# Reordering the first stage of a graph layer: two products held back, signs in halves, adj halves moved ahead, loads gated later

## The chip, the cores and the metric

The kernel runs on one core of a Trainium2 chip. The metric is the device time of one execution in microseconds (us), the median of three runs. Beside it stands one profiled execution, whose trace gives each instruction's start and length on TensorE (PE, with its weight loads PEld), VectorE (DVE), ScalarE (ACT), GpSimd (POOL) and SyncE (SP), and each transfer's issue and landing.

## The reference

Two graph layers over 4096 nodes with 512 features each. Only the first layer's product is touched by the change:

```python
def _L0_gnn_ref(x, support, weight):
    bw = _bin_sign(weight)            # sign
    ba = _bin_sign_z(x)               # max(sign, 0)
    xw = ba @ bw.T
    out = support @ xw                # support is adj, 4096 x 4096
    return jax.nn.relu(out)
...
x = _layernorm(x + _L0_gnn_ref(x, adj, L0_gnn_weight), axis=-1)
x = _layernorm(x + _L1_gnn_ref(x, adj, L1_gnn_weight, L1_gnn_bias, L1_gnn_node_w, L1_gnn_edge_w), axis=-1)
```

The second layer is an attention layer: h = x @ edge_w, a masked softmax over h @ h.T, and the product of adj times that attention with x @ weight.

## The kernel before

The 4096 nodes are cut into 32 row blocks of 128 (NB) and into 8 groups (NG) of 512 nodes, that is of four blocks (BG). The first layer runs in two stages. The second layer (from about 490 us on) uses a seven-product scheme for its large products and a planner for its own order; nothing of it is changed.

The first stage, up to about 55 us, builds xw, and meanwhile TensorE already uses each finished part of xw for two output row blocks, 0 and 4 (the list `early`), in the two accumulators acc 0 and acc 1. Its steps for a group g are these:

- `load_x(g)` (L182 to L186) loads the transposed x of the group, 1 MB, on SP's queue. `load_a(g, n)` (L188 to L193) loads adj of the group against early block n, 256 KB, on the same queue. For some of them a one-element memset on VectorE writes the tile first, so that the load must wait until VectorE has come that far in its own order.
- `signs_x(g)` makes the 0/1 signs on VectorE. Two blocks share one number: `over` is 2^11 for a positive element of the later block (L201), and `ba` is the sign of the earlier block plus that (L204). For group 0 this goes quarter by quarter as x and w0 land (L212, L213, and L210 for the weight's signs on ScalarE).
- `product(g, j)` multiplies ba by the weight's signs, four matmuls (L225). One product serves two blocks, j and j + 2.
- `taken(g, j)` separates the two by adding and taking away a large constant: L232 on ScalarE (us), L234 on VectorE (xw of block j), L235 on ScalarE (xw of block j + 2).
- `split(g, n)` splits adj of half n into hi, rounded to fp32r on ScalarE (L243), and lo, the rest, on VectorE (L244). hi and lo tiles have two buffers each, and one pair of tiles holds both halves of a group.
- `follow(g, n, cs)` adds hi times xw and lo times xw to acc n for the blocks cs of the group (L250, L252), two matmuls for each block.

For VectorE, ScalarE and TensorE the order of the program is the order in which these calls are written out by hand. SP's queue is in the hands of the framework's scheduler, which puts a load as early as its waits let it, so SP's order is not the written one. The loads draw on pools: adj halves on `rows` with four buffers, x on `stream` with three (w0 holds one at first).

After the stage, L308 and L310 load two vectors, node_w and bias, as tiles nw_b and bias_b of 128 partitions: each partition reads the same 2 KB row. They are used from 59 us on. The second stage then runs over the other 30 row blocks, each with 64 matmuls (L450, L451), the hi and lo split of its adj rows (L440, L442), and the layer norm of finished blocks between.

The written order of the first stage around the change is this (before the loop over g, then the loop):

Of the kernel before, what the change touches and what calls it, by code (L numbers as in the profile page):

```python
# [15 lines left out]
ALU = mybir.AluOpType  # L16
AX = mybir.AxisListType

P = 128
# [3 lines left out]
TWO = 2.0**11  # L23
# [6 lines left out]
def kernel(  # L30
# [13 lines left out]
    nc = tc.nc  # L44
# [114 lines left out]
    with (  # L159
# [19 lines left out]
        halves = [slice(h * (W // 2), (h + 1) * (W // 2)) for h in range(2)]  # L179

        def load_x(g):
            xts[g] = stream.tile([P, KD, W], F32, name="xt", tag="stream")  # L182
            if g == 1:
                nc.vector.memset(xts[g][:, 0, 0:1], 0.0)
            if g:
                nc.sync.dma_start(xts[g], x_t[:, ts(g, W)].rearrange("(k p) n -> p k n", p=P))  # L186

        def load_a(g, n):  # L188
            a = rows.tile([P, BG, P], F32, name="a0", tag="rows")
            if not g and n:  # L190
                nc.vector.memset(a[:, 0, 0:1], 0.0)
            nc.sync.dma_start(a, adj_t[early[n], :, ts(g, BG), :])
            split_a[g, n] = a  # L193

        def signs_x(g):
            xt = xts.pop(g)
            ba = wp.tile([P, KD, W // 2], F32R, name="ba", tag="quarter", bufs=2)
            over = wp.tile([P, KD, W // 2], BF16, name="over0", tag="scr")
            rights_s[g] = ba
            if g:  # L200
                nc.vector.tensor_scalar(over, xt[:, :, halves[1]], 0.0, TWO, ALU.is_gt, ALU.mult)  # L201
                yield
                for j in range(2):
                    nc.vector.scalar_tensor_tensor(  # L204
                        ba[:, :, ts(j, P)], xt[:, :, ts(j, P)], 0.0, over[:, :, ts(j, P)], ALU.is_gt, ALU.add
                    )
                    yield
                return
            for k in range(KD):
                nc.scalar.activation(bw[:, k, :], w0[:, k, :], AF.Sign, scale=-1.0)  # L210
                a, b = (xt[:, k, h] for h in halves)
                nc.vector.tensor_scalar(over[:, k, :], b, 0.0, TWO, ALU.is_gt, ALU.mult)  # L212
                nc.vector.scalar_tensor_tensor(ba[:, k, :], a, 0.0, over[:, k, :], ALU.is_gt, ALU.add)  # L213
                yield

        def zeros(n):
            for _ in range(n):
                nc.tensor.matmul(idle, warm[:, :P], warm, start=True, stop=True)
# [3 lines left out]
        def product(g, j):  # L222
            pw = pws[g, j] = ps_mm.tile([P, D], F32, name="pw", tag="mm")
            for k in range(KD):
                nc.tensor.matmul(pw, rights_s[g][:, k, ts(j, P)], bw[:, k, :], start=(k == 0), stop=(k == KD - 1))  # L225
                if g == 0 and (not j or k == KD - 1):
                    zeros(2)

        def taken(g, j):
            pw = pws.pop((g, j))  # L230
            u = us[:, j, :]
            nc.scalar.activation(u, pw, AF.Identity, bias=shift[:, 0:1])  # L232
            b = g * BG + j
            nc.vector.scalar_tensor_tensor(xw[:, b, :], u, SHIFT, pw, ALU.subtract, ALU.subtract)  # L234
            nc.scalar.activation(xw[:, b + BG // 2, :], u, AF.Identity, bias=shift[:, 1:2], scale=-1.0 / TWO)  # L235

        def split(g, n):
            if not n:
                hi = sp.tile([P, QC, P], F32R, name="hi", tag="hi")
                lo = sp.tile([P, QC, P], F32R, name="lo", tag="lo")  # L240
                split_a[g] = hi, lo
            (hi, lo), a = split_a[g], split_a.pop((g, n))
            nc.scalar.copy(hi[:, ts(n, BG), :], a)  # L243
            nc.vector.tensor_sub(lo[:, ts(n, BG), :], a, hi[:, ts(n, BG), :].bitcast(F32))  # L244

        def follow(g, n, cs=(0, 2, 1, 3), apart=False):
            hi, lo = split_a[g]
            for c in cs:
                kb = g * BG + c
                nc.tensor.matmul(accs[n], hi[:, n * BG + c, :], xw[:, kb, :], start=(kb == 0), stop=False)  # L250
                if not apart:
                    nc.tensor.matmul(accs[n], lo[:, n * BG + c, :], xw[:, kb, :], start=False, stop=(kb == NB - 1))  # L252
            for c in cs if apart else ():
                kb = g * BG + c
                nc.tensor.matmul(accs[n], lo[:, n * BG + c, :], xw[:, kb, :], start=False, stop=False)

        with tc.manual_schedule(
            engines={mybir.EngineType.DVE, mybir.EngineType.Activation, mybir.EngineType.PE}
        ):
            load_x(0)  # L260
            for k in range(KD):
                nc.sync.dma_start(w0[:, k, :], w0_t[ts(k, P), :])
                nc.scalar.dma_start(xts[0][:, k, :], x_t[ts(k, P), :W])
            load_a(0, 0)
            nc.scalar.activation(us[:, 0, 0:1], eps, AF.Sign)
            idle = ps_mm.tile([P, D], F32, name="idle", tag="mm")
            accs.extend(ps_tr.tile([P, D], F32, name="acc0", tag="tr") for _ in early)
            zeros(WARM)
            for k, _ in enumerate(signs_x(0)):
                if k == 1:  # L270
                    load_a(0, 1)
                    load_x(1)
            product(0, 0)
            split(0, 0)
            taken(0, 0)
            product(0, 1)
            split(0, 1)
            taken(0, 1)
            for _ in signs_x(1):
                pass  # L280
            follow(0, 0, (0, 2))
            follow(0, 1, (0, 2), True)
            follow(0, 0, (1, 3))
            follow(0, 1, (1, 3))
            for g in range(NG - 1):
                if g:
                    follow(g, 0)
                for n in range(2):
                    load_a(g + 1, n)
                if g + 2 < NG:  # L290
                    load_x(g + 2)
                for j in range(2):
                    product(g + 1, j)
                if g:
                    follow(g, 1)
                ahead = signs_x(g + 2) if g + 2 < NG else iter(())
                split(g + 1, 0)
                taken(g + 1, 0)
                next(ahead, None)
                taken(g + 1, 1)  # L300
                for _ in ahead:
                    pass
                split(g + 1, 1)
            for n in range(2):
                follow(NG - 1, n)

# [1291 lines left out]
    over = big.tile([P, KD * N], F32, name="over", tag="large")  # L1598
# [129 lines left out]
```

## Time and profile before

| what | us |
|---|---|
| median of 3 runs (1912.49 to 1913.65) | 1913.15 |
| the profiled execution | 1913.24 |
| its span, from first to last instruction | 1911.4 |
| TensorE busy in it | 1898.2 |
| VectorE busy | 1456.9 |
| ScalarE busy | 1024.4 |
| first product with adj (L250) | 12.24 |
| first product of the second stage (L450) | 55.49 |

The span is 1.84 us shorter than the execution's time; what is before the first and after the last instruction is in the difference. The granted clock of TensorE is 0.999 over the span. A row of a timeline gives an instruction's start, its length, engine, line and tiles, and in brackets how long the engine had been idle before it and what it had waited for. A matmul's length is longer than its distance to the next one, because matmuls overlap. A transfer's time is from its issue on the queue to the landing of its last byte.

### The profile page before, as it was taken

How to read it: one execution, taken by the hardware profiler on the slowest of the kernel's cores; microseconds unless marked ns; L12 is line 12 of the kernel's file. 1: busy time of each engine (PE TensorE's matmuls, PEld its weight loads, DVE VectorE, ACT ScalarE, POOL GpSimd, SP SyncE). 2: the span in 40 equal slices, each digit the busy share in tenths (PEclk: the TensorE clock that was granted, in tenths of full speed). 3: DMA queues.
4: the chain of work that ended last, by engine and by line, in shares of the span. 5: the costliest groups of instructions: out<-in, count | busy, mean ns of one | idle time of the engine just before them, and what ended most of it. 6: DMA issues, size and time to landing. Idle time of an engine off the chain costs nothing.

```text
span 1911.4 us, 20674 instructions
## 1 busy us (share of the span) xinstructions
PE 1898.2 (99%) x6886; PEld 1234.3 (65%) x6886; DVE 1456.9 (76%) x2230; ACT 1024.4 (54%) x1647; POOL 310.4 (16%) x449
## 2 busy tenths in 40 slices
PE   9999999999999999999999999999999999999998
PEld 6888888888644555555555556666666666656646
DVE  7777677776866567686864887898879988898947
ACT  6433333333212567666777656666676567667731
POOL 0133132231421111111110111111111111110100
PEclk9999999999999999999999999999999999999999
DMA  9889898898595378577784877887777877787731
GB/s 320 298 323 357 306 342 325 324 360 309 183 303 204 123 290 319 187 255 274 293 320 152 322 287 287 288 296 285 275 276 285 295 276 276 264 308 265 282 114 55
DMA packets 143914, 520.94 MB, mean 273 GB/s; under 512 B 15040, under 2 KB 15040, under 8 KB 136128
## 3 DMA queue, kind: packets, MB, share of 16 engines
q1 hardware_dynamic: 64368, 235.43, 36.2%
q0 software_dynamic: 67632, 248.54, 34.0%
q10 hardware_dynamic: 11808, 35.66, 5.1%
q8 instruction: 54, 0.88, 0.2%
q14 instruction: 52, 0.43, 0.1%
HBM read 397.93 MB, written 121.63 MB: 272 GB/s over the span
## 4 chain that ended last, share of the span: by engine, by line
PE 94%; DVE 3%; issue 1%; ACT 1%; DMA 1%; ACTq 0%; POOL 0%; POOLq 0%; DVEq 0%
PE bank L1279 36%; PE seven L869 12%; PE acc L450 11%; PE acc L451 11%; PE pe L733 6%; PE seven L101 5%; PE po L1429 4%; PE pt L695 3%; PE inner L832 2%; PE acc L250 1%; PE pt L410 1%; PE acc L252 1%; PE pw L225 1%; PE bank L1429 0%; DMA s_d<-slot 0%
## 5 line engine op out<-in xcount | busy, mean ns | idle before, releaser
L1279 PE MATMUL bank<-lent,lop 128*128 128x256 f32 (+1 forms) x1496 | 483.3, 473 | 0.3
L1279 PEld LDWEIGHTS bank<-lent,lop 128*128 128x128 f32 x1496 | 283.8, 190 | 167.4 <-issue 140.1
L450 PE MATMUL acc<-xw,hi 128*128 128x512 f32 x960 | 376.4, 392 | 0.0
L451 PE MATMUL acc<-xw,lo 128*128 128x512 f32 x960 | 374.1, 390 | 0.0
L1279 PE MATMUL bank<-slot,lop 128*128 128x512 f32 (+1 forms) x800 | 286.6, 503 | 1.0 <-DVE slot L1060 0.6
L440 ACT CAST hi<-at 128x1024 fp32r<-128x1024 f32 x120 | 126.5, 1054 | 203.2 <-PE acc L450 146.7
L1279 PEld LDWEIGHTS bank<-slot,lop 128*128 128x128 f32 x800 | 151.5, 190 | 115.9 <-issue 101.4
L1290 ACT COPY over<-bank 128x512 f32<-128x512 f32 x200 | 116.2, 585 | 200.0 <-PE bank L1279 196.0
L451 PEld LDWEIGHTS acc<-xw,lo 128*128 128x128 f32 x960 | 180.3, 188 | 36.8
L450 PEld LDWEIGHTS acc<-xw,hi 128*128 128x128 f32 x960 | 180.2, 188 | 36.8
L442 DVE TENSOR_TENSOR lo<-at,hi 128x1024 fp32r<-128x1024 f32 x120 | 147.6, 1230 | 66.3 <-ACT hi L440 65.9
L733 PE MATMUL pe<-hT 128*128 128x512 f32 (+3 forms) x384 | 132.1, 486 | 0.0
L657 DVE CUSTOM_DVE_ANT_0 line<-lent,slot 128x512 f32<-128x512 bf16 x140 | 90.3, 688 | 54.9 <-ACT slot L696 29.0
L666 ACT ACTIVATE line<-line,nmax_c 128x512 f32<-128x512 f32 x160 | 114.7, 722 | 21.2 <-DVE nmax_c L657 20.8
L1441 DVE SCALAR_TENSOR_TENSOR xb<-po,f,xb 128x256 f32<-128x256 f32 x84 | 40.3, 480 | 74.8 <-PE po L1429 74.7
L733 PEld LDWEIGHTS pe<-hT 128*128 128x128 f32 x384 | 64.6, 191 | 41.4 <-issue 33.8
L1048 DVE CUSTOM_DVE_ANT_1 lent<-lent,line 128x2048 f32<-128x2048 f32 x39 | 88.7, 2283 | 0.0
L1252 ACT COPY bank<-over 128x512 f32<-128x512 f32 x144 | 86.7, 603 | 0.0
L695 PEld LDWEIGHTS pt<-ident,lent 128*128 128x128 f32 x418 | 52.4, 141 | 44.8 <-issue 34.8
L1051 ACT ACTIVATE lent<-lent 128x2048 f32<-128x2048 f32 x39 | 74.9, 1920 | 7.9 <-DVE lent L1048 7.6
L1054 ACT ACTIVATE slot<-slot 128x2048 f32<-128x2048 f32 x37 | 71.1, 1923 | 7.6 <-DMA slot<-in_adj_t_dram 7.6
L696 ACT COPY slot<-pt 128x512 f32<-128x512 f32 (+3 forms) x123 | 68.3, 556 | 12.3 <-PE pt L695 12.2
(297 smaller groups left out, 3019.0 us busy)
## 6 DMA issues: line engine op xcount, KB each, us to landing
lop<-lop_d SPq DMA_DIRECT2D x154, 512.0 KB, 4.5
at<-in_adj_t_dram SPq DMA_DIRECT2D x60, 1024.0 KB, 7.3
slot<-in_adj_t_dram POOLq DMA_DIRECT2D x39, 1024.0 KB, 8.0
lent<-s_d POOLq DMA_DIRECT2D x38, 1024.0 KB, 7.8
s_d<-slot POOLq DMA_DIRECT2D x30, 1024.0 KB, 8.9
lent<-in_adj_t_dram POOLq DMA_DIRECT2D x25, 1024.0 KB, 8.0
lent<-in_adj_dram SPq DMA_DIRECT2D x48, 512.0 KB, 4.9
s_d<-lent POOLq DMA_DIRECT2D x48, 512.0 KB, 6.1
```

The source lines that it names most:

```text
L101: nc.tensor.matmul(banks[bank][q], lop(m, q)[k], rop(m)[k], start=(first and k == 0), stop=(k == K - 1), skip_group_check=not first,)
L440: nc.scalar.copy(hi, aq)
L442: nc.vector.tensor_sub(lo, aq, hi.bitcast(F32))
L450: nc.tensor.matmul(acc, hi[:, c, :], xw[:, kb, :], start=(kb == 0), stop=False)
L451: nc.tensor.matmul(acc, lo[:, c, :], xw[:, kb, :], start=False, stop=(kb == NB - 1))
L657: nc.vector.tensor_tensor_reduce(line, mask, src, -1.0, HUGE, ALU.add, ALU.min, accum_out=nmax_c[:, b, c : c + 1])
L666: nc.scalar.activation(line, line, AF.Exp, bias=nmax_c[:, b, c : c + 1], scale=-1.0, accum_out=sum_c[:, b, c : c + 1])
L695: nc.tensor.transpose(pt[:, j, :], src[:, ts(j, P)], ident)
L733: nc.tensor.matmul(pe[:, lo * P :], hT[:, k, ts(A * BG + i, P)], hT[:, k, (B * BG + lo) * P : (B + 1) * W], start=(k == 0), stop=(k == KD ...
L869: nc.tensor.matmul(ps, left[m][:, k, q, :], right[m][:, k, :], start=(first and k == 0), stop=(k == KD // 2 - 1), skip_group_check=not first,)
L1279: nc.tensor.matmul(ps, lop[:, k, :], rop[:, k, :], start=start, stop=(k == K - 1), skip_group_check=True)
L1290: nc.scalar.copy(self.to(), self.bank[:, : self.w])
```

## The change

Five things change, all in the first stage.

1. In `load_a`, the memset that gates a load is now written for adj half 1 of group 0 and for adj half 0 of group 1 (`g + n == 1`), before for the first of these alone. Both adj loads of group 1 are written together with `load_x(1)`, after the third quarter of group 0's signs; `load_x(1)` stood after the second quarter, and the adj loads of group 1 stood in the loop.
2. For the groups after the first, `signs_x` makes `over` in two halves of 4 x 128 elements, each just ahead of the half of ba that uses it, instead of one of 1024.
3. The last block of group 0 on acc 1 (two matmuls, hi and lo) comes behind group 1's sign products instead of ahead of them.
4. Group 1's products are reordered: block 0 of acc 1 comes between the pairs (0, 2) and (1, 3) of acc 0, and the rest of acc 1 follows after group 2's sign products in the order 2, 1, 3.
5. Both halves of group 1's adj are split ahead of `taken(1, 0)`; for the other groups half 1 stays behind `taken(g, 1)`.

```diff
         def load_a(g, n):
             a = rows.tile([P, BG, P], F32, name="a0", tag="rows")
-            if not g and n:
+            if g + n == 1:
                 nc.vector.memset(a[:, 0, 0:1], 0.0)
             nc.sync.dma_start(a, adj_t[early[n], :, ts(g, BG), :])
...
             if g:
-                nc.vector.tensor_scalar(over, xt[:, :, halves[1]], 0.0, TWO, ALU.is_gt, ALU.mult)
-                yield
                 for j in range(2):
+                    nc.vector.tensor_scalar(
+                        over[:, :, ts(j, P)], xt[:, :, ts(2 + j, P)], 0.0, TWO, ALU.is_gt, ALU.mult
+                    )
+                    if not j:
+                        yield
                     nc.vector.scalar_tensor_tensor(
...
             for k, _ in enumerate(signs_x(0)):
                 if k == 1:
                     load_a(0, 1)
+                elif k == 2:
                     load_x(1)
+                    for n in range(2):
+                        load_a(1, n)
...
-            follow(0, 1, (1, 3))
+            follow(0, 1, (1,))
             for g in range(NG - 1):
+                if g == 1:
+                    follow(1, 0, (0, 2))
+                    follow(1, 1, (0,))
+                    follow(1, 0, (1, 3))
+                elif g:
+                    follow(g, 0)
                 if g:
-                    follow(g, 0)
-                for n in range(2):
-                    load_a(g + 1, n)
+                    for n in range(2):
+                        load_a(g + 1, n)
                 if g + 2 < NG:
                     load_x(g + 2)
                 for j in range(2):
                     product(g + 1, j)
-                if g:
-                    follow(g, 1)
+                follow(g, 1, {0: (3,), 1: (2, 1, 3)}.get(g, (0, 2, 1, 3)))
                 ahead = signs_x(g + 2) if g + 2 < NG else iter(())
                 split(g + 1, 0)
+                if not g:
+                    split(1, 1)
                 taken(g + 1, 0)
                 next(ahead, None)
                 taken(g + 1, 1)
                 for _ in ahead:
                     pass
-                split(g + 1, 1)
+                if g:
+                    split(g + 1, 1)
```

## The prediction

> **What bounds the kernel now.** I read the page's head first, then busy time by stretch, then the first stretch instruction by instruction on TensorE, VectorE, ScalarE and SP's queue, and last the transfers with their landings. Head, and busy time by stretch (stretch, length, then busy us and count of PE, PEld, DVE, ACT, POOL, then granted clock, DMA share, GB/s):
>
> ```profile
> PE 1898.2 (99%) x6886; PEld 1234.3 (65%) x6886; DVE 1456.9 (76%) x2230; ACT 1024.4 (54%) x1647; POOL 310.4 (16%) x449
> ```
> ```profile
> 0.00:12.24 12.24, 9.43 (x30) 3.86 (x30) 4.67 (x16) 6.06 (x10) 0.74 (x6) 1.00 0.84 303
> 12.24:24.66 12.42, 11.70 (x50) 8.97 (x49) 10.02 (x16) 8.51 (x14) 0.00 (x0) 1.00 1.05 387
> 24.66:55.27 30.61, 30.61 (x137) 25.34 (x136) 23.91 (x38) 20.46 (x33) 0.00 (x0) 1.00 0.94 313
> ```
>
> TensorE is the bound of the program, and from 24.66 us on it has no gap in the stage that is changed. Holes lie only before. TensorE's timeline where they are (start, length, what, idle before and its releaser):
>
> ```profile
> 16.08 1.98 PE L225 MATMUL pw<-bw,ba 128*128 128x512 f32 x8
> 18.66 0.50 PE L250 MATMUL acc<-xw,hi 128*128 128x512 f32 x1 [0.60 <-DVE xw L234]
> 19.47 0.40 PE L252 MATMUL acc<-xw,lo 128*128 128x512 f32 x1
> 19.99 0.50 PE L250 MATMUL acc<-xw,hi 128*128 128x512 f32 x1
> 24.66 0.39 PE L250 MATMUL acc<-xw,hi 128*128 128x512 f32 x1
> ```
>
> Matmuls in a run start 0.227 us apart (eight in 1.81 us on the chain). Between 12.24, the first product with adj, and 24.66, the first of follow(2, 0), stand 48 matmuls: 48 x 0.227 = 10.88 us of the 12.42. **1.54 us is all that reordering could give back there**, 0.08% of the span. The two waits above are most of it: 0.76 us until xw of group 1's first pair (start 18.66 against 16.08 + 1.81 = 17.90) and 0.29 until the second (19.99 against 19.70). What 12.24 itself waits for is the start-up loads of x and w0, the last landing at 2.15 + 7.2 = 9.35 on the chain.
>
> The transfers decide the rest. SP's queue up to 14 us, and two stretches of DMA, 8 to 12 us and 42 to 43 us:
>
> ```profile
> 4.54 2.58 SPq L192 DMA_DIRECT2D a<-in_adj_t_dram  x3
> 7.21 0.38 SPq L186 DMA_DIRECT2D xt<-in_x_t_dram  x1
> 7.64 0.53 SPq L192 DMA_DIRECT2D a<-in_adj_t_dram  x1
> 38.67 0.42 SPq L308 DMA_DIRECT2D nw_b<-in_node_w_dram  x1
> ```
> ```profile
> DMA packets 825, 1.56 MB, mean 391 GB/s; under 512 B 62, under 2 KB 62, under 8 KB 825
> DMA packets 47, 0.09 MB, mean 94 GB/s; under 512 B 4, under 2 KB 4, under 8 KB 46
> ```
>
> In the first the DMA engines are full at 391 GB/s, and loads land one after another in the order of issue. The three adj loads issued at 4.54, 4.91 and 6.79 take 5.4, 5.7 and 4.5 us and so land at 9.9, 10.6 and 11.3; xt of group 1, issued at 7.21, takes 6.8 and lands at 14.0. So 256 KB cost 0.68 us of queue, 1 MB 2.7. In the second stretch, where nw_b and bias_b run, the same busy engines move 94 GB/s. The adj load before them lands at 38.20 + 3.9 = 42.1, nw_b at 38.67 + 6.2 = 44.9, bias_b at 39.14 + 7.2 = 46.3: **2.8 us for the first, 2.1 on average, for 256 KB each**. Both read one 2 KB row 128 times.
>
> **What the Trainium skill says.** "DMA: Bandwidth & Descriptors", Queues, rings and completion order: on each DMA engine descriptors are taken in ring order. The landings above agree, so a slow load delays all that SP issues after it. No page prices a source row read 128 times; the trace does. "VectorE: DVE Perf Modes", What auto-detection actually checks: a single-source operation in SBUF goes two elements a cycle if its outermost dimensions are even. Here L201's 1024 elements take 0.69 us and L212's 256 take 0.29, which is 0.16 + 0.00052 per element; a half of 4 x 128 elements costs 0.43. "TensorE: Matmul & The Clock Gate", What's actually happening: the clock halves after an idle window of about 3.4 us. TensorE's timeline has gaps of 0.98 and 0.54 us at 8 to 10 us and matmuls 0.23 apart after them; no gap that I expect is longer.
>
> **The change part by part.**
>
> *Loads.* Group 1's first adj load is now gated by a memset that follows the signs of x's third quarter, and xt(1) comes behind the same signs (L213, which ends at 8.67 on VectorE's timeline) instead of the second's (6.69). In the built program SP does not stay empty meanwhile: nothing holds nw_b, so it moves forward past 21 transfers to the sixth place, right where the first of group 1's adj loads stood. Its order is then w0's four, adj (0,0), **nw_b**, adj (0,1), xt(1), adj (1,0), adj (1,1), xt(2). The gate itself costs nothing: xt(1)'s turn on the DMA engines came at 11.3, 2.5 us after its new issue. Nor does it gain: adj loads stand behind all of w0 in SP's own ring, and x's last quarter lands at 9.35 beside w0's (9.15). What counts is nw_b for an adj load: 2.1 to 2.8 us for 0.68, so all later loads land d = 1.4 to 2.1 us later. I take d = 1.75: adj (0,1) lands at 13.0 (was 11.3), xt(1) at 15.7 (14.0), adj (1,0) and (1,1) at 16.4 and 17.1, xt(2) at 19.1 (17.4). nw_b's absence at 42 us is worth nothing, since no TensorE gap stands there.
>
> *Signs in halves, VectorE.* For each of seven groups one operation of 0.69 becomes two of 0.43, so 7 x 0.17 = 1.2 us in all. The first half of ba is ready 0.26 earlier, the second 0.19 later. In a steady group VectorE idles 1.01 of 5.44 us ahead of L234, and the second product starts 0.9 after the first, so this is hidden. Were a half one element a cycle, it would be 0.69 and +0.7 us a group, still under 1.01.
>
> *Adj halves of group 1 ahead of xw.* Two casts and two subtracts stand before us and xw of group 1 on ScalarE and VectorE. Behind the casts wait us and xw of group 1, and TensorE for these: with adj (1,1) at 17.1 the second cast ends at 17.75, 0.45 before us could start, so d has that much room there. The subtracts take 2 x 0.60 on VectorE ahead of xw, 0.3 us more than the cover gives (below).
>
> *Held products.* The same matmuls in another order: two (hi and lo of block 3 on acc 1, 0.45 us) go behind group 1's sign products to cover the first wait, two of group 1 go between its pairs for the second.
>
> *The walk with d = 1.75.* Cast of adj (0,1) at 13.0 to 13.7, then us 13.7 to 14.4, xw of the second pair on VectorE 14.4 to 15.1. TensorE: after the first four at 13.3 it stalls to 13.8 for the cast, 14.5 for the subtract, 15.2 for xw; six matmuls to 16.6. Signs from 15.8: 0.43, 0.69 to 16.95, 0.43, 0.69 to 18.0. Sign products 17.1 to 18.0 and 18.15 to 19.15. The held two end at 19.6. VectorE: two subtracts to 19.2, xw(1) to 19.8; TensorE resumes at 19.9. Four matmuls to 20.9, two to 21.35, four to 22.25 (the second xw is ready at 20.9), sign products of group 2 to 24.07, six to 25.43. Before was at the same point at 24.66: **+0.77 us**. The next group's inputs are in time: xw(2,0) at 24.85, xw(2,1) at 26.3 against its turn at 26.4. From there the matmul order is the old one, and ScalarE's and POOL's too, so the lag stays to the end.
>
> *The walk with d = 0*: signs from 14.06, products 15.63 to 17.45, held two to 17.9, xw(1) at 18.1, resume 18.2, and follow(2, 0) at 23.75: -0.9. So the stage shifts by about d - 0.95, and d = 1.4 to 2.1 gives +0.45 to +1.15.
>
> **Sum.** The profiled execution took 1913.24 us, 1.84 more than its span. 1911.4 + 0.8 + 1.84 = 1914.0; it stands 0.09 above the median of 1913.15, so 1913.9 beside that. A difference under 0.2% (3.8 us) is what a measurement of this kernel can't tell from no change.
>
> **The rivals.** *nw_b at the ordinary price.* At 10 us no second such row is read beside it, which speaks for a cheaper one; that its first 2.8 us were the slowest speaks against. Then -0.9: 1912.2. The holes close and still nothing measurable is won. *Slower by over 0.2%.* One mechanism: nw_b ahead of adj (0,1) holds the ring so long that the second half of group 0 starves TensorE. The lag is d - 0.95, so it decides from d = 4.8, nw_b taking 5.5 us. If it took its whole 6.2 us of issue to landing, d = 5.5 and +4.6: 1917.8. For it: reads of x and w0 are under way when it starts. Against: 94 GB/s is the lowest rate shown, and 256 KB at that are 2.8 us. *Faster by over 0.2%* would need 3.8 us from a stage with 1.54 to give; only a start-up load landing earlier could add, and none is moved ahead.
>
> **How the numbers follow.** My case (+0.2 to +1.8) has 0.62, ordinary nw_b 0.28, the slow rival 0.05; 0.05 is left for what I don't see, of which 0.02 faster and 0.01 slower by over 0.2%. Range: down to the ordinary price less the runs' own scatter of 0.6, 1911.6; up to d = 2.1 plus scatter, 1915.0, and on to a clock that halves once in the stalls (12 matmuls 0.43 apart at the start, some 4.7 us for half of that work: 2.3 more, an estimate), 1916.3. Faster 0.02, same 0.92, slower 0.06.
>
> **What would show it.** nw_b as SP's sixth transfer, landing about 12.3; adj (0,1) at 13.0, xt(1) at 15.7; TensorE gaps near 13.5 to 15.2 and 16.6 to 17.1, one of 0.3 near 19.6; follow(2, 0) from 25.4; no gap after. Wrong if adj (0,1) still lands near 11.3, if matmuls after 20 us start 0.43 apart, or if a new gap stands after 25.4.

## The result and the profile after

The changed kernel takes 1916.83 us (median of 15 runs, 1915.21 to 1918.69); the kernel before took 1913.15 beside it (15 runs). The ratio is 1.0018, 95% interval 1.0011 to 1.0026: 3.7 us slower. That is just inside the 0.2% that the prediction held for indistinguishable from no change, but with 15 runs on each side the interval excludes 1. The time lies 0.5 us above the upper end of the predicted range (1916.3). The profiled execution took 1916.83 us as well, with a span of 1915.1. A second measurement of the same kernel, called after_again below, gave 1916.90 (12 runs), ratio 1.0017 [1.0009, 1.0026].

The head of the page of the changed kernel, then its busy time by stretch (start:end, length, busy us and count of PE, PEld, DVE, ACT, POOL, granted clock, DMA share, GB/s):

```profile
PE 1898.4 (99%) x6886; PEld 1234.0 (64%) x6886; DVE 1460.4 (76%) x2238; ACT 1024.4 (53%) x1647; POOL 310.2 (16%) x449
```
```profile
12.24:27.15 14.91, 12.15 (x51) 8.80 (x49) 9.72 (x18) 8.27 (x14) 0.28 (x1) 1.00 1.00 347
27.15:58.00 30.85, 30.85 (x137) 25.53 (x136) 25.64 (x43) 20.88 (x34) 0.00 (x0) 1.00 0.86 306
```

TensorE's work is the same 6886 matmuls and the same 1898 us. From follow(2, 0) on there is again no gap in the stage. That point is now at 27.15 us and was at 24.66, so the first stage lost 2.5 us and all of it ahead of this point. TensorE's timeline of the changed kernel there (start, length, what, idle before and its releaser):

```profile
15.39 0.40 PE L255 MATMUL acc<-xw,lo 128*128 128x512 f32 x1
17.54 2.26 PE L228 MATMUL pw<-bw,ba 128*128 128x512 f32 x8 [1.75 <-DVE ba L207]
19.64 0.39 PE L253 MATMUL acc<-xw,hi 128*128 128x512 f32 x1
21.15 0.50 PE L253 MATMUL acc<-xw,hi 128*128 128x512 f32 x1 [0.88 <-DVE xw L237]
27.15 0.39 PE L253 MATMUL acc<-xw,hi 128*128 128x512 f32 x1
```

The two waits that the change was to cover were 0.60 us of idle time and 0.29 us by the late start. In their place stand one of 1.75 for group 1's signs and one of 0.88 for xw. VectorE's timeline shows what the signs and xw wait for in turn:

```profile
16.33 0.43 DVE L202 TENSOR_SCALAR over<-xt 128x512 bf16<-128x512 f32 x1 [2.28 <-DMA xt<-in_x_t_dram]
19.01 1.49 DVE L247 TENSOR_TENSOR lo<-a,hi 128x512 fp32r<-128x512 f32 x2 [0.46 <-ACT hi L246]
20.41 0.68 DVE L237 SCALAR_TENSOR_TENSOR xw<-us,pw 128x512 fp32r<-128x512 f32 x1
21.86 0.43 DVE L202 TENSOR_SCALAR over<-xt 128x512 bf16<-128x512 f32 x1 [0.77 <-DMA xt<-in_x_t_dram]
```

Three late loads are behind it: xt of group 1 holds the signs until 16.33; adj (1, 0) and (1, 1), landing at 18.3 and 19.1, hold the casts and so the two subtracts in front of xw (20.41); and xt of group 2 comes at 21.8. SP's queue of the changed kernel, in order of issue:

```profile
4.46 0.33 SPq L192 DMA_DIRECT2D a<-in_adj_t_dram  x1
4.83 0.43 SPq L321 DMA_DIRECT2D nw_b<-in_node_w_dram  x1
6.90 0.33 SPq L192 DMA_DIRECT2D a<-in_adj_t_dram  x1
8.75 0.38 SPq L186 DMA_DIRECT2D xt<-in_x_t_dram  x1
9.22 0.93 SPq L192 DMA_DIRECT2D a<-in_adj_t_dram  x2
10.25 0.57 SPq L186 DMA_DIRECT2D xt<-in_x_t_dram  x1
```

nw_b does stand sixth. But the adj load behind it, issued at 6.90, lands at 11.40 where the kernel before had 11.3. It is xt, issued 1.54 us later than before (8.75 against 7.21), that is late by more than this: 7.5 us from issue to landing instead of 6.8, so 16.2 instead of 14.0. The issue of xt, before and after (KB, us from issue to landing):

```profile
xt<-in_x_t_dram SPq DMA_DIRECT2D x1, 1024.0 KB, 6.8
```
```profile
xt<-in_x_t_dram SPq DMA_DIRECT2D x1, 1024.0 KB, 7.5
```

The transfers between 10 and 12 us, first of the kernel before, then of the changed one:

```profile
DMA packets 395, 0.78 MB, mean 391 GB/s; under 512 B 13, under 2 KB 13, under 8 KB 395
```
```profile
DMA packets 241, 0.46 MB, mean 232 GB/s; under 512 B 14, under 2 KB 14, under 8 KB 241
```

The DMA engines run short of work there: their busy share in these 2 us is 0.77 (near 1 is full), and 1.04 before, and they move 0.32 MB less, which is 0.8 us at 391 GB/s. Later the rate is low again. Between 14 and 20 us, before and after:

```profile
DMA packets 1183, 2.32 MB, mean 387 GB/s; under 512 B 49, under 2 KB 49, under 8 KB 1183
```
```profile
DMA packets 939, 1.81 MB, mean 301 GB/s; under 512 B 57, under 2 KB 57, under 8 KB 939
```

That is another 0.51 MB, but here the engines are busy (0.97 of the time, 1.05 before), so it is slower transfers and not a lack of them. Counted only until xt lands at 16.2, all that is missing against 391 GB/s comes to some 0.57 MB, or 1.4 of the 2.2 us by which xt is late (an estimate from the rates by stretch); the rest is not placed. The slow stretch goes on after xt's landing, and xt of group 2 comes 4.4 us late (21.8 against 17.4).

The second place where time goes is the end of the program. The last output write, issued at 1908.08 in the kernel before and at 1911.04 in the changed one, is 2.96 us late when it starts and 3.6 late when it lands. The transfers around the issue of that write, before and after (name, count, KB, us from issue to landing; of the changed kernel also the instruction queue):

```profile
out_dram<-slot SPq DMA_DIRECT2D x1, 256.0 KB, 2.0
```
```profile
q14 instruction: 1, 0.01, 14.9%
...
out_dram<-slot SPq DMA_DIRECT2D x1, 256.0 KB, 2.7
```

So the profiled executions differ by 2.5 us of the first stage, 0.7 of the last write, and 0.5 that build up between the two places, less than by which single executions of one kernel differ (1912.2 to 1916.8 us in the kernel before).

### The profile page after: what moved, and what is told of

Same layout as the page of the kernel before. It is cut to its first block, busy times and chain, and to the rows that moved or that the text cites. A ratio compares the mean times of both kernels' runs of the same rounds, so it can differ in the third digit from the quotient of the medians.

```text
span 1915.1 us, 20684 instructions
## 1 busy us (share of the span) xinstructions
PE 1898.4 (99%) x6886; PEld 1234.0 (64%) x6886; DVE 1460.4 (76%) x2238; ACT 1024.4 (53%) x1647; POOL 310.2 (16%) x449
## 4 chain that ended last, share of the span: by engine, by line
PE 93%; DVE 3%; DMA 2%; issue 1%; ACT 1%; ACTq 0%; POOL 0%; SPq 0%; DVEq 0%; POOLq 0%
PE bank L1292 36%; PE seven L882 12%; PE acc L464 11%; PE acc L463 11%; PE pe L746 6%; PE seven L101 5%; PE po L1442 4%; PE pt L708 3%; PE inner L845 2%; DMA xt<-in_x_t_dram 1%; PE pt L423 1%; PE acc L253 1%; PE acc L255 1%; PE pw L228 1%; PE bank L1442 0%
## 5 line engine op out<-in xcount | busy, mean ns | idle before, releaser
L709 ACT COPY slot<-pt 128x512 f32<-128x512 f32 (+3 forms) x123 | 68.3, 556 | 12.3 <-PE pt L708 12.2
```

## The experiments

"Lag" is how much later TensorE starts follow(2, 0) (or its neighbour in the old order) than in the kernel before. Each median stands beside a median of the kernel before on the same chip, which was between 1913.14 and 1913.61 in all of them.

### Which half of the change costs: a_old_loads and d_new_loads

The first is the changed kernel with the gate and the three loads where they had been; the second is the kernel before with the new gate and the new places of the loads, and nothing else.

```diff
a_old_loads, against the changed kernel
-            if g + n == 1:
+            if not g and n:
...
-                elif k == 2:
                     load_x(1)
-                    for n in range(2):
-                        load_a(1, n)
...
-                if g:
-                    for n in range(2):
-                        load_a(g + 1, n)
+                for n in range(2):
+                    load_a(g + 1, n)
```

> The changed kernel with every load as it was before (gates, places, nw_b at the end); the new order of products, signs and splits stays. If the loads alone made the change slow (nw_b in the queue, or xt(1) issued late), the first stage closes the holes: follow(2, 0) starts near 23.8 us (24.7 before, 27.2 in the changed kernel) and the time is 0.5 to 1 us under before. If the new order itself costs, follow(2, 0) starts at 25.5 or later and the time is at least 1 us over before.

> The kernel before with the loads alone as changed (gates, and so nw_b as sixth); products, signs and splits in the old order. Both theories of the loads say at least 2 us over before, with xt(1) near 16.2 us. The theory that the new order costs says 0 to 1 us over before.

a_old_loads: 1912.99 us, ratio 0.9996 [0.9988, 1.0005], lag -0.8. xt of group 1 is issued at 7.31 and lands at 14.1. The same matmuls in the new order, with halves of signs, held products and the adj halves ahead, do close the waits, for 0.8 us, which the whole time doesn't tell from nothing.

d_new_loads: 1916.6 us, ratio 1.0015 [1.0008, 1.0021]. The loads alone, under the old order of products, cost 3.1 us. In its profiled execution something more is to be seen. Busy time by stretch, then two lines of TensorE's timeline:

```profile
20.12:23.53 3.41, 1.68 (x6) 1.11 (x7) 1.89 (x5) 2.50 (x5) 0.00 (x0) 1.00 0.95 338
23.53:26.94 3.41, 3.41 (x10) 2.62 (x9) 1.87 (x4) 0.46 (x1) 0.00 (x0) 0.50 0.53 191
```
```profile
23.04 0.50 PE L250 MATMUL acc<-xw,hi 128*128 128x512 f32 x1 [1.62 <-DVE xw L234]
24.53 3.12 PE L225 MATMUL pw<-bw,ba 128*128 128x512 f32 x8
```

After 3.41 us in which TensorE was busy for half, the granted clock is 0.50 for the next 3.41: eight matmuls take 3.12 us instead of 1.98. That loses 1.7 us (an estimate, half of 3.41). This profile is one of only 2 of the kernel's 21 executions with a mean clock under 0.999, so the 3.1 us of the median are not from it. More on this below.

### The gate or nw_b: e_xt_late_alone, c_nwb_early, f_xt_early, b_vectors_late

e_xt_late_alone moves one call in the kernel before; c_nwb_early moves only nw_b, to the sixth place; f_xt_early takes only the late `load_x(1)` out of the changed kernel; b_vectors_late takes only nw_b out of the sixth place of the changed kernel, by gating it and bias_b behind VectorE's work in group 5.

```diff
e_xt_late_alone, against the kernel before
                 if k == 1:
                     load_a(0, 1)
+                elif k == 2:
                     load_x(1)
c_nwb_early, against the kernel before (the tile and its load leave their old place)
+            nc.sync.dma_start(nw_b, ...)        # right behind load_a(0, 0)
f_xt_early, against the changed kernel
                     load_a(0, 1)
-                elif k == 2:
                     load_x(1)
+                elif k == 2:
                     for n in range(2):
                         load_a(1, n)
b_vectors_late, against the changed kernel (tiles and loads leave their old place)
             for g in range(NG - 1):
+                if g == 5:
+                    for v, vec in ((nw_b, node_w), (bias_b, bias)):
+                        nc.vector.memset(v[:, 0:1], 0.0)
+                        nc.sync.dma_start(v, ...)
```

> The kernel before with one edit: xt(1) is gated by the third quarter's signs, not the second's. adj loads, nw_b and all orders as before. If the late gate lets the DMA engines run dry, xt(1) lands at 15.7 us or later although the load ahead of it lands at 11.2, TensorE's first sign product of group 1 starts at 17.2 or later (16.1 before), and the time is 1.5 to 3 us over before. If the gate is free, as the prediction had it, xt(1) lands near 14.0 and the time is within 0.5 us of before.

> The kernel before with nw_b loaded as the sixth transfer on SP; gates and all orders as before. If nw_b's place is the cause, xt(1) lands at 15.5 us or later and the time is 1 to 2.5 us over before. If the late gate of xt(1) is, nw_b is worth only its 256 KB (0.7 us of queue) and the time is 0 to 0.7 us over before.

> The changed kernel with one edit: xt(1) back behind the second quarter's signs; nw_b is still the sixth transfer, adj of group 1 behind xt(1). If the late gate is most of the loss, xt(1) lands at 14.5 to 15.6 us, follow(2, 0) starts at 24.3 to 25.7 (27.2 in the changed kernel), and the time is 0 to 1.2 us over before. If nw_b's place is most of it, the time stays 2.5 us or more over before.

> The changed kernel with nw_b and bias_b held by a memset on VectorE until the end of the first stage; SP then puts adj (1,1) where nw_b was, and xt(1) keeps its late gate. If nw_b's place made the change slow, xt(1) lands near 14.0 us, follow(2, 0) starts at 23.8 to 24.5 and the time is 0 to 1 us under before. If the late gate of xt(1) did, xt(1) lands at 16 us or later and the time stays 2 us or more over before.

| run | median us, ratio to before | xt (1): issue, landing | lag |
|---|---|---|---|
| e_xt_late_alone | 1915.29, 1.0008 [1.0002, 1.0015] | 9.02, 16.46 | +2.1 |
| c_nwb_early | 1914.81, 1.0007 [0.9999, 1.0015] | 7.47, 15.58 | +1.2 |
| f_xt_early | 1914.72, 1.0007 [0.9999, 1.0016] | 7.44, 15.22 | +0.3 |
| b_vectors_late | 1916.54, 1.0015 [1.0009, 1.0022] | 9.01, 16.11 | +1.2 |

Gating xt behind the third quarter of signs is enough by itself to make the kernel before slower. Its transfers between 10 and 12 us, the issue of xt, and the place where TensorE pays, in three views of e_xt_late_alone:

```profile
DMA packets 216, 0.42 MB, mean 209 GB/s; under 512 B 12, under 2 KB 12, under 8 KB 216
```
```profile
xt<-in_x_t_dram SPq DMA_DIRECT2D x1, 1024.0 KB, 7.4
```
```profile
18.03 2.11 PE L225 MATMUL pw<-bw,ba 128*128 128x512 f32 x8 [1.82 <-DVE ba L204]
```

The same dry stretch as in the changed kernel (busy share 0.74), with no nw_b near. Sign products start at 18.03 instead of 16.08, and the lag stays. With old loads the same window shows this (a_old_loads):

```profile
DMA packets 383, 0.76 MB, mean 381 GB/s; under 512 B 11, under 2 KB 11, under 8 KB 383
```

The dry stretch alone doesn't explain the slow transfers that follow in the changed kernel: between 14 and 20 us e_xt_late_alone moves 366 GB/s, and c_nwb_early and f_xt_early, with nw_b sixth but xt early, 394 each. The three profiles with both and no idle matmuls (the changed kernel twice, d_new_loads) move 297 to 304.

nw_b in the sixth place costs about what the prediction said of it, where xt is early: in c_nwb_early nw_b lands at 10.89 and adj (0, 1) at 12.88 (1.6 us late), xt 1.6 us late; in f_xt_early xt is 1.2 us late and the lag is +0.3, which is the prediction's d - 0.95 for d = 1.25. The medians of these two are 1.3 and 1.1 us over, with intervals that just include no change.

With a_old_loads (-0.8) and the changed kernel (+2.3 to 2.5) the four lags make a square: from -0.8, nw_b's place adds 1.1 (f_xt_early), xt's late issue 2.0 (b_vectors_late), both together 3.1 to 3.3. (Three of the four also have adj (1, 0) gated and moved; in b_vectors_late adj (1, 1) takes nw_b's place.) So the two costs add up in the stage, and the late issue is the larger. In medians the late issue is the difference of the changed kernel and f_xt_early, 2.1 to 2.2 us. f_xt_early stands 1.1 over the kernel before and a_old_loads 0.5 under; of these 1.6 us, 0.9 is the late write at the end, treated below, that one has and the other has not.

### Is it the distance of the gate, or the order: i_xt_late_behind_adj and h_both_held

In i_xt_late_behind_adj, the kernel before with xt as late as in e_xt_late_alone, both adj loads of group 1 go ahead of it so that the queue has 256 KB more to do. h_both_held is an attempt at a better version: the changed order, with four products held back instead of two, xt directly behind adj (0, 1) after the second quarter, both adj loads of group 1 gated behind it, and both vectors late as in b_vectors_late.

```diff
i_xt_late_behind_adj, against the kernel before (the loop's adj loads then only if g)
                 if k == 1:
                     load_a(0, 1)
+                    for n in range(2):
+                        load_a(1, n)
+                elif k == 2:
                     load_x(1)
h_both_held, against the changed kernel (vectors as in b_vectors_late)
-            if g + n == 1:
+            if g + n == 1 or g == 1:
...
-                elif k == 2:
                     load_x(1)
...
-            follow(0, 1, (1,))
...
-                follow(g, 1, {0: (3,), 1: (2, 1, 3)}.get(g, (0, 2, 1, 3)))
+                follow(g, 1, {0: (1, 3), 1: (2, 1, 3)}.get(g, (0, 2, 1, 3)))
```

> The kernel before with xt(1) gated late (third quarter), but now both adj loads of group 1 stand ahead of it on SP, 256 KB more than in the run where the gate alone was late. If the late gate hurts because the DMA engines run dry between the last adj load's bytes and xt(1)'s first bytes (some 2 us after its issue), the extra load fills that time: xt(1) lands at 14.6 to 15.5 us, earlier than the 16.5 it had with less ahead of it, and the time is 0.3 to 1.2 us over before. If a 1 MB load simply needs 7 us from its issue, or each load ahead costs its bytes, xt(1) lands at 16.2 to 17.2 and the time is 1.7 us or more over.

> A version meant to beat both: the changed order, four products held back instead of two, xt(1) behind the second quarter's signs and directly behind adj (0,1), both adj loads of group 1 behind xt(1), nw_b and bias_b at the end of the stage. If xt(1)'s landing and the cover of the wait for xw are what bound the stage, xt(1) lands near 13.3 us, follow(2, 0) starts at 23.2 to 23.6 and the time is 0.8 to 1.5 us under before. If the two adj splits ahead of xw bound it, follow(2, 0) is no earlier than 23.9, as with the old loads.

i_xt_late_behind_adj: 1915.31 us, ratio 1.0011 [1.0005, 1.0018], lag +1.5; xt issued at 9.09 lands at 15.88, 6.8 us later. It falls between the two expectations. Still, xt lands 0.6 us earlier than in e_xt_late_alone with 256 KB more to move ahead of it, which would be 0.68 us at the full rate. The rate between 10 and 12 us is 341 GB/s, not 209. So the dry queue is a cost in its own right, seen in one profile of each. The medians don't show it: this kernel stands 1.9 us over the kernel before, e_xt_late_alone 1.7.

h_both_held: 1912.57 us, ratio 0.9995 [0.9987, 1.0003], lag -0.9. xt lands 6.0 us after its issue, at 13.3, the earliest of all. In the stage it is ahead of the kernel before by as much as a_old_loads is, not by the 1.1 to 1.5 us that were expected of its earlier loads (follow(2, 0) starts at 23.8, near the 23.9 expected if the two splits of adj bind), and by too little for the whole time to show. No order that was tried won more than 0.9 us in the stage.

### Does the clock halve: after_again, j_clock_kept, k_vectors_late_clock_kept, b_vectors_late_again

d_new_loads made it likely that the same happens in some executions of the changed kernel. j_clock_kept puts nine idle matmuls into the two waits, of the kind that the kernel has at its start; their results go nowhere. k_vectors_late_clock_kept is b_vectors_late with the first six of them.

```diff
j_clock_kept, against the changed kernel
             follow(0, 1, (1,))
+            zeros(6)
             for g in range(NG - 1):
                 if g == 1:
+                    zeros(3)
                     follow(1, 0, (0, 2))
```

> The changed kernel again, for a second profile. If the lag of the first stage is made by the loads' order alone, follow(2, 0) starts within 0.5 us of 27.2 again; if it hangs on how the DMA packets fall, it moves by 1 us or more.

> The changed kernel with nine idle matmuls on zeros in TensorE's two gaps (six ahead of group 1's sign products, three ahead of its first product with adj); their result goes nowhere. The loads stay late. If a clock that halves in some executions after these gaps makes part of the loss, hardly a run shows a granted clock under 0.999 and the time is 0.4 to 1 us under the changed kernel's. If the gaps cost only their own length, the time stays within 0.3 us of the changed kernel's 1916.8.

> The kernel with nw_b and bias_b held to the end of the first stage again, for a second profile. Its first profile lagged 1.2 us at 23 us and its median 3.1. If the stage's lag varies between executions, the second profile lags 2 us or more there; if it is 1.2 again, the rest arises later.

> The kernel with nw_b and bias_b held to the end of the stage, with six idle matmuls on zeros in TensorE's gap ahead of group 1's sign products; their result goes nowhere. Without them its stage lagged 1.1 to 1.2 us in two profiles, its median was 3.1 over before, and 9 of 21 runs showed a granted clock under 0.999. If the halved clock makes the difference, no more than 2 runs show it now and the time is 1 to 2 us over before. If it doesn't, the time stays 2.5 us or more over before although the clock is whole, and where the rest arises stays open.

The mean granted clock of the span was under 0.999 in 11 of 27 executions of the changed kernel and in 9 of 21 of b_vectors_late; in none of the 21 of j_clock_kept and the 21 of k_vectors_late_clock_kept, and in 8 of the 228 executions of the kernel before that were measured beside the experiments. So some 4 of 10 executions have a lower clock, and idle matmuls in the waits end it. That it is a halving like the one in d_new_loads is not shown: no profile of the changed kernel caught one. Nor does the length of the gap decide: e_xt_late_alone has one of 1.82 us, longer than the changed kernel's 1.75, and a lower clock in 1 of 21. What tips it stays open.

What it is worth is less sure. Executions with the lower clock have a median above the others' by 0.3 us in the first measurement of the changed kernel, 1.9 in after_again and 1.2 in b_vectors_late. j_clock_kept took 1916.09, ratio 1.0015 [1.0009, 1.0022], 0.8 us under after_again, but its lag is smaller too (+1.8 against +2.3), so 0.3 is left for the clock. k_vectors_late_clock_kept took 1915.89, ratio 1.0012 [1.0005, 1.0018], against 1916.54 of b_vectors_late: 2.5 us over the kernel before, with a whole clock. Its lag of +1.5 and the late write of 0.8 make most of that. The second profile, b_vectors_late_again, was of one execution: 1915.07 us, lag +1.1, last write late.

### The late write at the end

In the profiles so far the last write takes 2.0 us in one set of kernels (before, a, c, d, e, h, i) and 2.7 to 2.9 in the other (the changed kernel, after_again, b, f, j, k). Each profile of the second set, and none of the first, has one transfer of q14, the queue that the profile calls instruction, in the last 6 us. Where such a transfer falls should depend on how many instructions an engine has run, so the first attempt was to add instructions on VectorE, of which the changed kernel has 8 more.

```diff
l_changed_plus8, m_before_plus9, n_before_plus4: written behind the first stage
+        count = wp.tile([P, 1], F32, name="count")
+        for _ in range(8):                      # 9, 4
+            nc.vector.memset(count, 0.0)
l2_changed_plus8, m2_before_plus9: the same without a tile of its own
+        for _ in range(8):                      # 9
+            nc.vector.memset(warm[:, 0:1], 0.0)
```

> The changed kernel with eight one-column memsets on VectorE at the end of the first stage; nothing else. If the 0.7 to 0.9 us at its very end come from the transfer of instructions that falls beside the last output write, that transfer comes at an earlier point of the program, as in h_both_held (2241 VectorE instructions, transfer over 10 us before the end): last two writes 2.0 us each, no q14 transfer in the last 6 us, and a median 0.5 to 0.8 us below the changed kernel's, 1916.0 to 1916.4. If the late writes belong to the first stage's reordering in another way, they keep taking 2.6 to 2.9 us and the median stays at 1916.8 to 1917.1.

> The kernel before with nine one-column memsets on VectorE at the end of the first stage, so 2239 VectorE instructions, between the changed kernel's 2238 and b_vectors_late's 2240. If the instruction transfer decides, it falls in the last 6 us, the last write takes 2.6 to 2.9 us, and the median is 0.6 to 1.0 above before. If not, the last write takes 2.0 us and the median is within 0.3 of before.

> The kernel before with four such memsets, 2234 VectorE instructions, fewer than the 2237 of a_old_loads which has no instruction transfer at the end. Both theories: last write 2.0 us, median within 0.3 of before; this is the price of the memsets themselves.

All three came out 12 us slower than the kernels they were made from, the one with four memsets too: 1929.14, 1925.03 and 1925.04 us, ratios to before 1.0084 [1.007, 1.0098], 1.006 [1.0047, 1.0074] and 1.0061 [1.0048, 1.0073]. That is the new tile, not the memsets, and is shown under the last heading. The times of these say nothing of the question. The scheduler also moved the memsets: in the profiles they run near 1.2 us, and in the next two runs at 12 to 24 us, not behind the stage. Repeated on a tile that was there:

> The changed kernel with eight one-column memsets on VectorE at the end of the first stage, now onto a tile that is there already, so that no tile moves in SBUF. If the instruction transfer beside the last write costs the 0.7 to 0.9 us at the end, and eight more VectorE instructions bring it forward (2246 against h_both_held's 2241): last two writes 2.0 us each, no q14 transfer in the last 6 us, median 0.5 to 0.8 below the changed kernel's, 1916.0 to 1916.4. If the late writes belong to the reordered stage in another way: 2.6 to 2.9 us as before and a median of 1916.8 to 1917.1. The run with an added tile had a q14 transfer in the last 6 us at 2246 as well, which speaks for a position that does not go by VectorE's count alone.

> The kernel before with nine such memsets, 2239 VectorE instructions. If VectorE's count places the transfer and the transfer delays the last write: q14 transfer in the last 6 us, last write 2.6 to 2.9 us, median 0.6 to 1.0 above before. If the count doesn't place it, as 2239 with an added tile had none: last write 2.0 us and median within 0.3 of before, and the correlation with the transfer is then all there is.

l2_changed_plus8: 1917.08, ratio 1.0018 [1.001, 1.0025]; last write 2.8, the transfer still beside it. m2_before_plus9: 1913.58, ratio 1.0001 [0.9993, 1.0009]; 2.0, no transfer. VectorE's count doesn't place it. ScalarE's does: in the built programs that were counted, with waits and branches, ScalarE has 1905 or 1906 instructions in the kernels without the transfer at the end, 1907 in all with it, and 1908 in h_both_held, whose transfer falls over 10 us before the end. (The traces hold 207 more of them in each run that was counted, and by their counts the rule fits every run.) The last run gives the kernel before that count.

```diff
o_before_scalar2, against the kernel before
         nc.sync.dma_start(bias_b, ...)
+        for c in range(2):
+            nc.scalar.copy(bias_b[:, c : c + 1], bias_b[:, c : c + 1])
```

> The kernel before with two one-column copies on ScalarE more (bias_b onto itself), which makes 1907 instructions for ScalarE in the built program, waits included. All six programs with late last writes that were counted have 1907 there; the kernels with 1905, 1906 or 1908 have none. If the transfer of ScalarE's instructions beside the last write makes it late: a q14 transfer in the last 6 us, last write 2.6 to 2.9 us, median 0.5 to 1.0 above before, with the first stage as before. If the reordered stage makes it late in another way: 2.0 us, no such transfer, median within 0.3 of before.

It took 1915.67 us, ratio 1.0013 [1.0005, 1.0021]. The transfers of its last 0.5 us of issuing and the page's count of the queue:

```profile
out_dram<-slot SPq DMA_DIRECT2D x1, 256.0 KB, 2.6
```
```profile
q14 instruction: 53, 0.43, 0.1%
```

The transfer is there (53 where the kernel before has 52), and the last two writes take 2.5 and 2.6 us, with the first stage's order untouched. So the late write belongs to the instruction transfer and not to the reordering. The median says less than hoped, because the copies also held ScalarE until bias_b had landed and opened two gaps on TensorE:

```profile
47.66 0.50 PE L250 MATMUL acc<-xw,hi 128*128 128x512 f32 x1 [0.54 <-ACT xw L235]
48.96 0.50 PE L250 MATMUL acc<-xw,hi 128*128 128x512 f32 x1 [0.56 <-DVE xw L234]
```

By the start of the second stage the gaps and the slower starts around them cost 1.7 us (the same matmul runs at 57.48 instead of 55.72, and 0.1 of this lag was there at 24.66). These and the 0.6 of the write make the 2.3 by which the median is longer. 4 of its 15 executions had a lower clock too, so the median by itself doesn't price the write; the profile does.

## Why the prediction was wrong

**The failed step.** The prediction said: "The gate itself costs nothing: xt(1)'s turn on the DMA engines came at 11.3, 2.5 us after its new issue." It read the landing of the load ahead as the moment when the engines come free, and took 2.5 us of slack. e_xt_late_alone refutes it: the gate alone, without anything else of the change, makes xt land 2.5 us later and the kernel 1.7 us slower by its median (0.4 to 2.9 by its interval). f_xt_early shows it from the other side: taking the late issue out of the changed kernel gives 2.1 us back.

Two things were wrong in the step. The engines are done with a load before it counts as landed. In e_xt_late_alone the adj load ahead of xt lands at 11.24, but already between 10 and 11 us the engines are short of work (busy share and GB/s are the last two numbers; e_xt_late_alone, then the kernel before):

```profile
10.00:11.00 1.00, 0.83 (x5) 0.53 (x5) 0.44 (x2) 0.87 (x2) 0.15 (x1) 1.00 0.72 180
```
```profile
10.00:11.00 1.00, 0.73 (x4) 0.49 (x4) 0.54 (x2) 0.78 (x2) 0.00 (x0) 1.00 1.05 393
```

And a load that is issued needs time until its first bytes move: in the kernel before the very first load is issued at 0.74 us, and the engines' first traffic comes near 2. The Trainium skill has a fixed part, "DMA: Bandwidth & Descriptors", Anatomy of one DMA: about 2.0 us of setup and completion handling for a transfer that GpSimd issues. The loads here are issued by SP. The 2.0 us of a 256 KB output write on SP's queue at the end, of which 0.7 would be its bytes at 391 GB/s, leave 1.3 (an estimate). How the 2.5 us of slack divide between the two ends was not measured.

**nw_b in the sixth place** was seen rightly, and its size d = 1.4 to 2.1 holds where xt is early (1.6 in c_nwb_early, 1.2 in f_xt_early, a little under the low end). In the changed kernel it didn't show where it was looked for: nw_b landed at 10.5, not 12.3, and adj (0, 1) at 11.4, not 13.0, so the stalls foretold at 13.5 to 15.2 didn't come. The time was lost behind, with xt. This also speaks against the prediction's picture of the queue, in which a slow load delays all that SP issues after it and nothing else. f_xt_early differs from the changed kernel only in that xt is issued earlier (7.44 against 8.75), and there adj (0, 1), which stands ahead of xt, landed at 12.53 instead of 11.40. A load behind delayed a load ahead; how is open.

**xt (2)** was put at 19.1, "later by d". Its own order listed nw_b as one more 256 KB ahead of xt (2), which makes 19.8 by the prediction's own prices. It landed at 21.8, behind the slow stretch described above.

**The walk's rules** held. The order alone was said to give 0.9 back at d = 0; a_old_loads gave 0.8. f_xt_early followed d - 0.95. The halves of signs cost 0.43 each as stated. The lag that the stage leaves was carried on (2.5 us at 27.15 and at the start of the second stage, 3.0 at the last write). That nw_b's absence at 42 us is worth nothing was not tested by itself.

**The clock.** The prediction kept a single halving for the upper end of the range (2.3 us, an estimate) but said that no gap it expected was longer than 0.98. The gate made one of 1.75. The Trainium skill, "TensorE: Matmul & The Clock Gate", What's actually happening, names an idle window of about 3.4 us; in d_new_loads 3.41 us that were half idle, with 1.62 us as the longest gap, went before a halving, which lost some 1.7 us. In the changed kernel the lower clock is in 4 of 10 executions, and its share of the median is not known.

**The range.** Its upper end is 1915.0 and 2.3 more by its own words, which is 1917.3; 1916.3 was written, which is 2.3 on the central 1914.0. With 1917.3 the range would have held the measured time, but by luck, for the late issue that made most of it was put at nothing.

**The end of the program** was in no step: that a few more instructions on ScalarE bring a transfer of instructions beside the last write.

The sum: of the 3.7 us, the first stage takes 2.3 to 2.5 in two profiles at the full clock, the late write 0.7 to 0.9. Together they are 3.1 in the profile of either measurement, whose medians are 3.7 and 3.3 over, so 0.2 to 0.5 is left. The lower clock, 0.3 to 1.9 us in 4 of 10 executions, would add 0.1 to 0.8 to a mean (an estimate); its share in the median was not separated. Why the transfers run at 301 GB/s between 14 and 20 us, with the same sizes of packets, is not settled by any run here.

## What to carry to other kernels

The landing of the load ahead doesn't say how late the next one may be issued. Here the engines stayed full with an issue 4 us before that landing (7.21 against 11.3). With 2.95 us (i_xt_late_behind_adj, 9.09 against 12.04) the rate between 10 and 12 us fell to 341 GB/s, and with 2.2 and 2.65 (e_xt_late_alone, the changed kernel) to 209 and 232. Look at the transfer rate around the place first, and when a gate is moved, ask what the scheduler will pull into the slot that it leaves. When all the gain in reach is 1.5 us, a moved load can cost more than that.

## What the hardware showed beside

A new tile of 4 bytes per partition, put ahead of others, made the program 12 us slower. Busy time by stretch, the kernel before and then n_before_plus4, in the second stage:

```profile
200.00:490.00 290.00, 290.00 (x1317) 240.04 (x1316) 209.52 (x339) 93.98 (x115) 82.82 (x115) 1.00 0.89 323
```
```profile
200.00:490.00 290.00, 290.00 (x1285) 234.40 (x1284) 205.43 (x332) 91.59 (x113) 79.21 (x113) 1.00 0.88 319
```

In the same 290 us, at the same clock and with no gap, TensorE does 1285 matmuls instead of 1317: 0.226 us each instead of 0.220. The hi and lo tiles, allocated after the new one, would shift by its 4 bytes. That their address is what matters was not tried. Memsets alone, nine of them on an old tile, cost nothing (m2_before_plus9).

The other surprise is the late write: where one 8 KB transfer of instructions falls beside the last output writes, the last two take 0.5 to 0.9 us longer, so that two more ScalarE instructions at 46.7 us can show at 1911. How so small a transfer delays them was not looked into.
